# Turning gathered blocks by transposes, with the adjacency part added by VectorE and a woven VectorE order, in a two-layer graph network

## The chip, the cores and the metric

The kernel runs on one core of a Trainium2 chip. The metric is the device time of one execution in microseconds (us). Times are compared by medians of several executions; the profiles are single executions.

## What is computed

Sixteen graphs of N = 1024 nodes and 256 features pass through two layers; each layer ends in a layer norm of the sum with its input. Layer 0 is one attention head with batch norms. The change lies in layer 1, which has four heads and the 0/1 adjacency `adj`, sparse in these inputs:

```python
coefs_adj = softmax(adj)                      # the same for all heads
def head(...):                                # for each of the 4 heads
    fts = inputs @ W
    f1 = fts @ w1h + b1h
    f2 = fts @ w2h + b2h
    logits = f1[:, :, None] + f2[:, None, :]
    coefs_logits = softmax(leaky_relu(logits, 0.2) + bias_mat)   # bias_mat: -1e9 where adj is 0
    coefs = ah * coefs_logits + (1.0 - ah) * coefs_adj
    vals = coefs @ fts + bh
    return elu(vals + inputs)
out = layernorm(x + mean over heads)
```

## The kernel before, in words

Layer 0 runs first (to about 900 us of the profile), then layer 1; the constants of layer 1 (`constants1`) are made in pieces during layer 0.

Layer 1 does not multiply by the full matrices. For each graph it lists which nodes are joined to small blocks of target nodes, fetches just those rows of x, and gathers. A graph has K = 8 groups of 128 target nodes, each five blocks (NB) of QB = 25 nodes plus three shared "last" rows. For a block, `gather` (L1817, TensorE) makes `pu`: 125 rows of 256, that is 25 weighted sums for each of the four heads and 25 plain sums over the neighbours (the adjacency part). ScalarE divides each row by its sum of weights (L1883, `s`). `turn` (L1889, TensorE) then turns and mixes: for each of five blocks, `s` is the weight operand and the constant MX (125 x 100) the moving one, so that one product gives, with features down and the 25 nodes of each head across, alpha times the head's rows plus (1 - alpha) times the adjacency rows. ScalarE copies the 128 x 500 result `pt` to `sT` (`turned`, L1899). `linear` (L1912) multiplies `sT` by the heads' weights W1s; VectorE adds x as it evicts (`add`, L1920), ScalarE takes exponentials (`exps`, L1926), VectorE makes elu and the sum over heads (`sum`, L1933 to L1941), and `mean` (L1948), `squares` (L1955), `span`, `power` (POOL), `close` (L1976) and `store` are the layer norm. All matrices are float32; a float32 matrix product is two TensorE instructions, a float32 transpose one.

A unit is one group and one half: two heads in `linear`, one half of the features in `turn`. There are 16 units per graph and 256 in all. The order of instructions on every engine is written out by hand, in one loop over units (`for n in range(-EARLY, len(units) + 12)`): iteration n issues different steps of different units, for example `add` of unit n-6, `turn` and `turned` of n-3, `linear` of n-5, `gather` of n. [...]

Beside the units stands the work that prepares the next graphs ("sides"). It is put at fixed iterations relative to a graph's first unit, by the tables AT, AT0 and AT1, and comes in four parts that `stand(part, n)` issues: 0 VectorE work, 1 TensorE work and what leads to it, 2 what follows (ScalarE, DMAs), 3 the weights of gathered rows (`weigh`). The steps that matter here: `words` and `worded` (TensorE `pc`, ScalarE's copy L325, VectorE's sum L331), `pick` and `picked` (48 and 8 small products into `po`, L1520, then VectorE L1530), `turn`, `residual` and `beside` of the graph (`pz`, L1690; VectorE's copy of `fs`, L1707), `norm`, `factors`, `raised` (VectorE makes `f`, L1750; ScalarE's exponentials from it, L1756 to L1761) and `scale` (eight ScalarE instructions, L1737). Most small TensorE results of the sides share two PSUM buffers (pool `ps_s`, tag "s"); `pt` has one buffer, `pv` two, `pu` three.

The body of the loop:

```python
do(n - 9, "power")
do(n - 6, "add")
stand(0, n)
do(n - 6, "exps")
do(n - 3, "turn", "turned")
do(n - 1, "invert")
do(n - 1, "norm")
stand(2, n)
...
do(n - 5, "linear")
...
stand(3, n)
do(n - 6, "sum")
do(n - 7, "squares")
```

Of the kernel before, what the change touches and what calls it, by code (L numbers as in the profile page):

```python
# [12 lines left out]
I32 = mybir.dt.int32  # L13
# [14 lines left out]
def kernel(  # L28
# [184 lines left out]
    MX = cpool.tile([P, H, QB], F32, name="MX")  # L213
    ibits = cpool.tile([P, QB], I32, name="ibits")
# [16 lines left out]
    def constants1(wp):  # L231
# [4 lines left out]
        for oc in range(C):  # L236
# [4 lines left out]
        MY = wp.tile([P, H, QB], F32, name="MY")  # L241
        nc.vector.tensor_tensor(
            MX, ident[:, 0 : H * QB].rearrange("p (h q) -> p h q", h=H),
            al_bc.unsqueeze(2).to_broadcast([P, H, QB]), ALU.mult,
        )
        nc.vector.tensor_tensor(
            MY, ident[:, H * QB : QR].unsqueeze(1).to_broadcast([P, H, QB]),
            om_bc.unsqueeze(2).to_broadcast([P, H, QB]), ALU.mult,
        )
        nc.vector.tensor_tensor(MX, MX, MY, ALU.add)  # L250
        yield
        bits = wp.tile([P, QB], F32, name="bits")
        for i in range(QB):
# [9 lines left out]
            pick, ident[:, LO : LO + NB * QB].rearrange("p (q n) -> p n q", n=NB),  # L263
# [6 lines left out]
        rest = wp.tile([P, 3], F32, name="rest1")  # L270
        nc.vector.tensor_copy(rest[:, 0:LO], ident[:, 0:LO])
        nc.vector.tensor_copy(rest[:, LO:3], ident[:, P - 1 : P])
        last = wp.tile([P, K, 3], F32, name="last")
        nc.vector.tensor_tensor(
            last, rest.unsqueeze(1).to_broadcast([P, K, 3]),
# [35 lines left out]
        nc.sync.dma_start(W1s[0:1, 0], bias1[0:1])  # L311
# [714 lines left out]
    def dense(arm):  # L1026
# [25 lines left out]
        class Graph:  # L1052
# [157 lines left out]
            def spread(self):  # L1210
# [7 lines left out]
                ar = pk.tile([H * K, P], F32, tag="ar", name=f"ar_{self.b}", bufs=2)  # L1218
# [191 lines left out]
    with ExitStack() as l1:  # L1410
# [9 lines left out]
        class Lists:  # L1420
# [19 lines left out]
            def worded(self, hf):  # L1440
# [4 lines left out]
                words_copied(self.wd, self.pc, hf)  # L1445
                words_summed(self.wl, self.pc, hf)
# [16 lines left out]
            def placed(self):  # L1463

                b, pp = self.b, self.pp
                nc.vector.tensor_tensor(most, most, pp[:, K, :], ALU.max)
                pi = pk.tile([P, K, NQ], I32, tag="pi", name=f"pi_{b}", bufs=1)
                nc.vector.tensor_copy(pi, pp[:, 0:K, :])
                nc.vector.tensor_scalar(pi, pi, 15, None, ALU.bitwise_and)
                self.hi = pk.tile([P, K, NQ], FP16, tag="hi", name=f"hi_{b}", bufs=1)  # L1470
                nc.vector.tensor_tensor(self.hi, pp[:, 0:K, :], pi, ALU.subtract)
                nc.vector.tensor_copy(low[:, :, 0:NQ], pi)
# [15 lines left out]
            def high(self, part):  # L1488
# [3 lines left out]
                for i in range(4 * part, 4 * part + 4):  # L1492
# [3 lines left out]
                    )  # L1496

            def higher(self):
# [6 lines left out]
                )  # L1505
                nc.vector.tensor_tensor(
# [18 lines left out]
            def picked(self):  # L1525
# [7 lines left out]
                )  # L1533
                with nc.allow_low_precision(reason="one whole number and zeros"):
# [3 lines left out]
                nc.vector.tensor_scalar(  # L1538
# [630 lines left out]
```

## Time and profile before

| what | value |
|---|---|
| median of 3 executions (lowest, highest) | 2237.07 us (2195.85, 2263.55) |
| the profiled execution, and its span | 2269.36 us, 2267.5 us |
| TensorE products busy (PE) | 2058.0 us, 91% of the span |
| VectorE busy (DVE) | 1836.3 us, 81% |
| ScalarE busy (ACT) | 1453.9 us, 64% |
| GpSimd busy (POOL) | 1130.0 us, 50% |
| granted TensorE clock, mean over the span | 0.934 of full |
| `turn` L1889, products | 2560 instructions, 350.2 us, 286 ns each |
| `turned` L1899, ScalarE's copy | 256, 144.2 us, 563 ns each |
| `add` L1920, VectorE | 256, 175.1 us, 684 ns each |

A row of a group of instructions reads: line, engine, operation, out<-in with the program's names, shape, count; then busy time, the mean of one, and the idle time of the engine just before them with what released it. In a timeline a row reads: start, duration, engine, line, operation, number of instructions, and in brackets the idle time before it. A wait reads: engine, line, releaser, total time, times, longest.

### The profile page before, as it was taken

What the parts mean: (1) busy time and instruction counts of PE and PEld (TensorE: products, weight loads), DVE (VectorE), ACT (ScalarE), POOL (GpSimd) and SP (SyncE); (2) the same over time, 40 slices, a digit from 0 to 9 for tenths busy, and PEclk for the clock granted to TensorE, in tenths of its full rate; (3) what the DMA queues carried; (4) which work ended last, traced back from release to release, by engine and by line L of the source; (5) the groups of instructions that cost most, each with busy time, mean ns of one, the idle gap of its engine ahead of it and who ended that gap; (6) DMA issues with size and microseconds to landing.
All of it is one profiled execution on the core that took longest, in us unless ns stands there. A gap on an engine that the chain in (4) does not pass through costs nothing. (4 is left out here: it accounts for less than half of the span.)

```text
span 2267.5 us, 35993 instructions
## 1 busy us (share of the span) xinstructions
PE 2058.0 (91%) x12152; PEld 1594.8 (70%) x12152; DVE 1836.3 (81%) x4480; ACT 1453.9 (64%) x3192; POOL 1130.0 (50%) x1115
## 2 busy tenths in 40 slices
PE   7988799998699955999999999999999999999996
PEld 5846544444344434788888888888888888888885
DVE  3447999987599955889889889889889889889785
ACT  1236767665477733676776776776767767767674
POOL 1010266444140005666766757667667657666571
PEclk9997899998799966999999999999999999999998
DMA  7999479999997216765765756766756756756551
GB/s 237 319 180 214 108 173 219 186 161 203 177 226 186 93 59 217 194 168 182 194 170 171 197 169 173 196 165 172 203 161 164 215 155 170 208 164 169 132 143 33
DMA packets 321157, 398.42 MB, mean 176 GB/s; under 512 B 171791, under 2 KB 268099, under 8 KB 310595
## 3 DMA queue, kind: packets, MB, share of 16 engines
q1 hardware_dynamic: 268555, 250.01, 45.1%
q0 software_dynamic: 51840, 145.61, 26.4%
q8 instruction: 99, 1.62, 0.3%
q10 hardware_dynamic: 568, 0.40, 0.2%
q14 instruction: 95, 0.78, 0.1%
HBM read 326.70 MB, written 102.78 MB: 189 GB/s over the span
## 5 line engine op out<-in xcount | busy, mean ns | idle before, releaser
L1595 POOL DMA_INDIRECT xc<-xe_dram,ix x640 | 686.7, 1073 | 211.2 <-issue 182.2
L1912 PE MATMUL pv<-W1s,sT 128*128 128x256 f32 x2048 | 508.4, 393 | 0.4 <-ACT sT L1906 0.4
L887 PE MATMUL pa<-em,wh 128*128 128x512 f32 x1024 | 457.4, 605 | 10.4 <-DVE em L845 10.4
L1912 PEld LDWEIGHTS pv<-W1s,sT 128*128 128x128 f32 x2048 | 383.9, 198 | 45.1 <-ACT sT L1906 0.8
L1889 PEld LDWEIGHTS pt<-MX,s 125*128 125x128 f32 x2560 | 349.4, 203 | 29.0 <-ACT sT L1899 8.5
L887 PEld LDWEIGHTS pa<-em,wh 128*128 128x128 f32 x1024 | 195.8, 194 | 244.2 <-issue 240.1
L1889 PE MATMUL pt<-MX,s 125*128 125x100 f32 x2560 | 350.2, 286 | 4.3 <-ACT sT L1899 1.9
L1817 PE MATMUL pu<-xc,w 128*125 128x256 f32 x1280 | 346.7, 390 | 0.0
L1883 ACT ACTIVATE s<-pu,z 125x256 f32<-125x256 f32 x640 | 261.2, 474 | 79.7 <-DVE z L1875 53.3
L1926 ACT ACTIVATE m<-v,neg 128x512 f32<-128x512 f32 x256 | 183.9, 718 | 197.7 <-DVE v L1920 154.8
L97 POOL COPY mark<-em 1x1 f32<-1x1 f32 x48 | 162.4, 3384 | 224.3 <-DVE em L845 224.3
L1817 PEld LDWEIGHTS pu<-xc,w 128*125 128x125 f32 x1280 | 232.4, 192 | 34.4 <-issue 6.1
L1899 ACT COPY sT<-pt 128x500 f32<-128x500 f32 x256 | 144.2, 563 | 113.3 <-PE pt L1889 113.2
L1969 POOL TENSOR_TENSOR ors<-ors,mhalf 128x1 f32<-128x1 f32 x128 | 110.8, 866 | 196.4 <-DVE ors L1963 195.1
L839 ACT ACTIVATE e<-e,v,u 128x1024 f32<-128x1024 f32 x128 | 158.2, 1237 | 77.2 <-DVE e L833 73.0
L833 DVE SCALAR_TENSOR_TENSOR e<-e 128x1024 f32<-128x1024 f32 x128 | 155.3, 1214 | 59.2 <-ACT e L826 59.2
L826 ACT ACTIVATE e<-eb,c,s 128x1024 f32<-128x1024 f32 x128 | 157.5, 1232 | 54.8 <-DMA eb<-ec_dram 51.9
L1920 DVE TENSOR_TENSOR v<-pv,x 128x512 f32<-128x512 f32 x256 | 175.1, 684 | 16.1 <-PE pv L1912 15.9
L845 DVE TENSOR_TENSOR em<-e,mt 128x1024 f32<-128x1024 f32 x128 | 156.0, 1218 | 1.3 <-ACT e L839 1.3
L1690 PE MATMUL pz<-IW,h 128*128 128x136 f32 x512 | 89.9, 308 | 68.6 <-DVE fs L1707 38.1
L1690 PEld LDWEIGHTS pz<-IW,h 128*128 128x128 f32 x512 | 77.5, 205 | 83.5 <-issue 44.7
L853 DVE TENSOR_TENSOR sm<-sm,e 128x1024 f32<-128x1024 f32 x96 | 116.9, 1218 | 0.0
(331 smaller groups left out, 3276.1 us busy)
## 6 DMA issues: line engine op xcount, KB each, us to landing
x<-in_x_dram SPq DMA_DIRECT2D x32, 1024.0 KB
adj<-in_adj_dram POOLq DMA_DIRECT2D x64, 512.0 KB
A<-u_dram SPq DMA_DIRECT2D x128, 250.0 KB
rw<-adj SPq DMA_DIRECT2D x30, 1024.0 KB
xe_dram<-x SPq DMA_DIRECT2D x16, 1060.0 KB
h_dram<-hb SPq DMA_DIRECT2D x16, 1024.0 KB
h<-h_dram SPq DMA_DIRECT2D x16, 1024.0 KB
out_dram<-o SPq DMA_DIRECT2D x128, 128.0 KB
```

Of the source, the lines that this page charges most:

```text
L97: tc.keep_in_program_order(nc.gpsimd.tensor_copy(self.mark, data))
L826: nc.scalar.activation(e, ebs[b], AF.Identity, bias=c1[:, k, b : b + 1], scale=s1[:, k : k + 1])
L839: nc.scalar.activation(e, e, AF.Exp, bias=v2[:, k : k + 1], scale=u2[:, k : k + 1])
L887: nc.tensor.matmul(acc[b, hf, oc].rearrange("p k q -> p q k"), wh[b][:, k, oc * P : (oc + 1) * P], ems[b, k][:, hf * HALF : (hf + 1) * HAL ...
L1595: nc.gpsimd.indirect_dma_start(out=self.xc[:, i, :], out_offset=None, in_=xe_dram[g.b % 2], in_offset=bass.IndirectOffsetOnAxis(ap=g.l.ix[ ...
L1690: nc.tensor.matmul(pz[:, oc, :], self.h[:, oc, k * P : (k + 1) * P], IW[:, oc, :], start=True, stop=True,)
L1817: nc.tensor.matmul(pu[0:QR, 0:F], c.w[:, k].rearrange("p h q -> p (h q)"), c.xc[:, k, 0:F], start=(i == 0), stop=(i == len(OF[q]) - 1),)
L1883: nc.scalar.mul(f.s[0:QR, i], f.pu[i][0:QR, 0:F], f.z[0:QR, i : i + 1])
L1889: nc.tensor.matmul(self.pt[:, :, :, i], self.first.s[0:QR, i, self.hp * P : (self.hp + 1) * P], MX[0:QR], start=True, stop=True,)
L1912: nc.tensor.matmul(self.pv[:, hh, :], self.first.sT[:, fc, self.hp * HP + hh, :], W1s[:, fc, self.hp * HP + hh, :], start=(fc == 0), stop= ...
L1920: nc.vector.tensor_tensor(self.v2, self.pv, self.g.x[:, self.it].unsqueeze(1).to_broadcast([P, HP, F]), ALU.add)
L1926: nc.scalar.activation(self.m, self.v2, AF.Exp, bias=neg1, scale=1.0)
```

## The change

**Turn.** Four of the five blocks are no longer multiplied by MX. They are transposed on TensorE (against the identity), into a `pt` whose rows are four heads and the adjacency part, 25 nodes by four blocks. ScalarE copies the adjacency part to `sM` (128 x 100), and `turned` is now a VectorE addition of `sM` to the four heads as they leave PSUM (128 x 400). The fifth block still uses MX, once for both halves of the features, on every second unit (`turn_fifth`, into a `ps_s` buffer `pf`; copied by ScalarE in `turned_fifth`).

**Mixing weights.** (1 - alpha) goes into W1s and the bias, alpha / (1 - alpha) into the divisors of the four blocks (`part`, one small ScalarE instruction per unit) and into MX. `spread` uses a permutation matrix `by_block` in place of the identity. These constants are made in `constants1`.

**Moved to ScalarE.** `mean`, `means` and the scaling of the last rows in `gathered`.

**Order.** Many VectorE steps yield between their instructions, and `woven` issues the threads `weigh`, side part 0 and `sum` in turn, one instruction of each. In the loop `invert`, `turn` and `turned` come straight after `add`; `linear` and `turn_fifth` come before the woven part. In `weigh` the product comes ahead of the bit mask. For graph 1 the side step `turn` has its own times. Side steps that free PSUM come first in part 0.

The diff, cut to its core:

```diff
@@ -238,16 +240,40 @@
...
-        MY = wp.tile([P, H, QB], F32, name="MY")
+        om = wp.tile([P, 2, H], F32, name="om")
+        nc.vector.tensor_scalar(om[:, 0], om_bc, 0.0, FAINT, ALU.is_equal, ALU.mult)
+        nc.vector.tensor_tensor(om[:, 0], om[:, 0], om_bc, ALU.add)
+        nc.vector.reciprocal(om[:, 1], om[:, 0])
+        nc.vector.tensor_tensor(om[:, 1], om[:, 1], al_bc, ALU.mult)
         nc.vector.tensor_tensor(
             MX, ident[:, 0 : H * QB].rearrange("p (h q) -> p h q", h=H),
-            al_bc.unsqueeze(2).to_broadcast([P, H, QB]), ALU.mult,
+            om[:, 1].unsqueeze(2).to_broadcast([P, H, QB]), ALU.mult,
         )
         nc.vector.tensor_tensor(
-            MY, ident[:, H * QB : QR].unsqueeze(1).to_broadcast([P, H, QB]),
-            om_bc.unsqueeze(2).to_broadcast([P, H, QB]), ALU.mult,
+            MX, MX, ident[:, H * QB : QR].unsqueeze(1).to_broadcast([P, H, QB]), ALU.add,
         )
-        nc.vector.tensor_tensor(MX, MX, MY, ALU.add)
...
+        nc.vector.tensor_reduce(most_of[:, 0:1], apart.rearrange("p h q -> p (h q)"), AX.X, ALU.add)
+        nc.vector.tensor_reduce(most_of[:, 1:2], ident[:, H * QB : P], AX.X, ALU.add)
+        nc.vector.tensor_tensor(part, most_of[:, 0:1], most_of[:, 1:2], ALU.add)
...
@@ -308,7 +331,13 @@
...
         for fc in range(C):
             nc.vector.tensor_tensor(W1s[:, fc], W1s[:, fc], wl, ALU.subtract)
-        nc.sync.dma_start(W1s[0:1, 0], bias1[0:1])
+            nc.vector.tensor_tensor(
+                W1s[:, fc], W1s[:, fc], om[:, 0].unsqueeze(2).to_broadcast([P, H, F]), ALU.mult
+            )
+        nc.vector.tensor_tensor(
+            wl[0:1], bias1[0:1], om[0:1, 0].unsqueeze(2).to_broadcast([1, H, F]), ALU.mult
+        )
+        nc.sync.dma_start(W1s[0:1, 0], wl[0:1])
...
@@ -1443,6 +1472,7 @@
...
+                yield
                 words_summed(self.wl, self.pc, hf)
 
             def used(self):
@@ -1531,13 +1566,15 @@
...
+                nc.vector.tensor_scalar(
+                    V[:, NB:8].rearrange("p g a -> p (g a)"), po[:, 320:344], in8[:, 0:1], None, ALU.mult
+                )
+                yield
                 with nc.allow_low_precision(reason="one whole number and zeros"):
                     nc.vector.tensor_reduce(
                         V[:, 0:NB], t.rearrange("p g q a -> p g a q"), AX.X, ALU.add
                     )
-                nc.vector.tensor_scalar(
-                    V[:, NB:8].rearrange("p g a -> p (g a)"), po[:, 320:344], in8[:, 0:1], None, ALU.mult
-                )
+                yield
                 self.E = pk.tile([P, 8, 8, 16], FP16, tag="E", name=f"E_{b}", bufs=1)
                 nc.vector.tensor_tensor(
@@ -1606,15 +1643,9 @@
...
                 wi = flat.bitcast(I32)[:, a : a + (n - 1) * step + 1 : step]
-                mi = pk.tile([P, n, QB], I32, tag="mi" + self.big, name=f"mi_{self.nm}", bufs=2)
-                nc.vector.tensor_tensor(
-                    mi, wi.unsqueeze(2).to_broadcast([P, n, QB]),
-                    ibits.unsqueeze(1).to_broadcast([P, n, QB]), ALU.bitwise_and,
-                )
                 w = self.w = pk.tile(
                     [P, n, H + 1, QB], F32, tag="w" + self.big, name=f"w_{self.nm}", bufs=4 if n == NB else 2
                 )
-                nc.scalar.copy(w[:, :, H, :], mi)
                 A = g.A[self.u]
                 if self.u == K:
                     nc.vector.memset(w[:, :, 0:H, QB - 1 : QB], 0.0)
@@ -1627,10 +1658,19 @@
...
+                yield
+                mi = pk.tile([P, n, QB], I32, tag="mi" + self.big, name=f"mi_{self.nm}", bufs=2)
+                nc.vector.tensor_tensor(
+                    mi, wi.unsqueeze(2).to_broadcast([P, n, QB]),
+                    ibits.unsqueeze(1).to_broadcast([P, n, QB]), ALU.bitwise_and,
+                )
+                nc.scalar.copy(w[:, :, H, :], mi)
+                yield
                 nc.vector.tensor_tensor(
                     w[:, :, 0:H, :], w[:, :, 0:H, :],
                     xc[:, :, F1 + H : WB].unsqueeze(3).to_broadcast([P, n, H, QB]), ALU.max,
                 )
+                yield
                 nc.vector.tensor_tensor(
                     w[:, :, 0:H, :], w[:, :, 0:H, :], mi.unsqueeze(2).to_broadcast([P, n, H, QB]), ALU.mult
...
@@ -1708,7 +1748,7 @@
...
             def means(self, hf):
                 mn = self.mv[:, 0, hf * KH : (hf + 1) * KH]
-                nc.vector.tensor_scalar(mn, mn, -1.0 / F, None, ALU.mult)
+                nc.scalar.mul(mn, mn, -1.0 / F)
...
@@ -1743,10 +1783,13 @@
+                yield
                 nc.vector.tensor_tensor(self.f, self.f, self.fs[:, :, 1], ALU.add)
+                yield
                 nc.vector.tensor_tensor(
                     self.f, self.f, self.rs[:, 1].unsqueeze(2).to_broadcast([P, K, 2 * H]), ALU.mult
                 )
+                yield
                 nc.vector.tensor_tensor(
@@ -1792,18 +1835,16 @@
...
             def spread(self):
                 self.pb = ps_s.tile([K * H, 2, P], F32, tag="s", name=f"pA_{self.b}")
-                nc.tensor.transpose(self.pb[:, 0], self.e.rearrange("p k h -> p (k h)"), ident)
-                nc.tensor.transpose(self.pb[:, 1], self.e2.rearrange("p h k -> p (h k)"), ident)
+                for i, e in enumerate(
+                    (self.e.rearrange("p k h -> p (k h)"), self.e2.rearrange("p h k -> p (h k)"))
+                ):
+                    nc.tensor.matmul(self.pb[:, i], e, by_block, start=True, stop=True)
 
             def spreaded(self):
                 n = NB * QB
                 self.ar = pk.tile([K * H, P], F32, tag="ar", name=f"ar_{self.b}", bufs=2)
-                nc.scalar.copy(
-                    self.ar[:, 0:n].rearrange("p (n q) -> p q n", n=NB),
-                    self.pb[:, 0, LO : LO + n].rearrange("p (q n) -> p q n", n=NB),
-                )
-                nc.scalar.copy(self.ar[:, n : n + LO], self.pb[:, 1, 0:LO])
-                nc.scalar.copy(self.ar[:, n + LO : P], self.pb[:, 1, P - 1 : P])
+                nc.scalar.copy(self.ar[:, 0:n], self.pb[:, 0, 0:n])
+                nc.scalar.copy(self.ar[:, n:P], self.pb[:, 1, n:P])
...
@@ -1827,7 +1868,7 @@
...
-                nc.vector.tensor_scalar(self.s[0:QR], self.pu[0:QR, 0:F], z[0:QR], None, ALU.mult)
+                nc.scalar.mul(self.s[0:QR], self.pu[0:QR, 0:F], z[0:QR])
 
...
@@ -1879,28 +1921,48 @@
...
+                lo, hi = (0, 3) if self.hp == 0 else (3, 4)
+                nc.scalar.mul(f.z[0:QR, lo:hi], f.z[0:QR, lo:hi], part[0:QR])
                 for i in self.blocks():
                     nc.scalar.mul(f.s[0:QR, i], f.pu[i][0:QR, 0:F], f.z[0:QR, i : i + 1])
 
             def turn(self):
 
-                self.pt = ps_t.tile([P, H, QB, NB], F32, tag="t", name=f"pt_{self.nm}")
-                for i in range(NB):
+                f = self.first
+                self.pt = ps_t.tile([P, H + 1, QB, NB - 1], F32, tag="t", name=f"pt_{self.nm}")
+                for i in range(NB - 1):
                     nc.tensor.matmul(
-                        self.pt[:, :, :, i],
-                        self.first.s[0:QR, i, self.hp * P : (self.hp + 1) * P],
-                        MX[0:QR], start=True, stop=True,
-                    )
+                        self.pt[:, :, :, i], f.s[0:QR, i, self.hp * P : (self.hp + 1) * P],
+                        ident[0:QR, 0:QR].rearrange("p (h q) -> p h q", h=H + 1),
+                        start=True, stop=True, is_transpose=True,
+                    )
+                if self.hp == 0:
+                    f.sT = pk.tile([P, C, H, SW], F32, tag="sT", name=f"sT_{self.nm}", bufs=2)
+                self.sM = pk.tile([P, (NB - 1) * QB], F32, tag="sM", name=f"sM_{self.nm}", bufs=2)
+                nc.scalar.copy(self.sM, self.pt[:, H].rearrange("p q n -> p (q n)"))
...
             def turned(self):
-                f, u = self.first, self.it
-                if self.hp == 0:
-                    f.sT = pk.tile([P, C, H, P], F32, tag="sT", name=f"sT_{self.nm}", bufs=2)
-                nc.scalar.copy(
-                    f.sT[:, self.hp, :, LO : LO + NB * QB],
-                    self.pt.rearrange("p h q n -> p h (q n)"),
-                )
+                rows = self.first.sT[:, self.hp, :, LO:SW].rearrange("p h (e j) -> p h e j", e=2)
+                nc.vector.tensor_tensor(
+                    rows[:, :, :, 0 : 2 * QB],
+                    self.pt[:, 0:H].rearrange("p h q n -> p h (q n)").rearrange("p h (e j) -> p h e j", e=2),
+                    self.sM.rearrange("p (e j) -> p e j", e=2).unsqueeze(1).to_broadcast([P, H, 2, 2 * QB]),
+                    ALU.add,
+                )
+
+            def turn_fifth(self):
                 if self.hp == 1:
+                    self.pf = ps_s.tile([P, C, H, QB], F32, tag="s", name=f"pf_{self.nm}")
+                    for fc in range(C):
+                        nc.tensor.matmul(
+                            self.pf[:, fc], self.first.s[0:QR, NB - 1, fc * P : (fc + 1) * P],
+                            MX[0:QR], start=True, stop=True,
+                        )
+
+            def turned_fifth(self):
+                if self.hp == 1:
+                    f, u, m = self.first, self.it, LO + 2 * QB
+                    nc.scalar.copy(f.sT[:, :, :, m : m + QB], self.pf)
                     sl = self.g.sl[:, :, :, 3 * u : 3 * u + 3]
                     nc.scalar.copy(f.sT[:, :, :, 0:LO], sl[:, :, :, 0:LO])
                     nc.scalar.copy(f.sT[:, :, :, P - 1 : P], sl[:, :, :, LO:3])
@@ -1933,10 +1995,13 @@
...
                 nc.vector.scalar_tensor_tensor(v, self.m, 1.0, v, ALU.min, ALU.max)
+                yield
                 nc.vector.tensor_tensor(v, g.acc, v, ALU.add)
+                yield
                 o = self.o = pk.tile([P, F], F32, tag="o", name=f"o_{nm}", bufs=4)
 
                 nc.vector.scalar_tensor_tensor(o, g.x[:, it, 0:F], float(H), v[:, 0], ALU.mult, ALU.add)
+                yield
                 self.mv = pk.tile([P, 2], F32, tag="omv", name=f"omv_{nm}", bufs=5)
                 nc.vector.tensor_tensor_reduce(
...
@@ -1945,9 +2010,7 @@
...
             def mean(self):
                 if self.hp == 1:
-                    nc.vector.tensor_scalar(
-                        self.mv[:, 0:1], self.mv[:, 0:1], -1.0 / F, None, ALU.mult
-                    )
+                    nc.scalar.mul(self.mv[:, 0:1], self.mv[:, 0:1], -1.0 / F)
...
@@ -2010,6 +2073,7 @@
...
         }
+        AT1['turn'] = (-18, -18, -17, -15, -15, -14, -14, -13)
 
...
@@ -2025,7 +2089,7 @@
...
                 first[n] += [each(f, *args)]
-                early[n + 1] += [each(then, *args)]
+                freed[n + 1] += [each(then, *args)]
 
...
@@ -2089,35 +2153,52 @@
...
+        def in_turn(steps):
+            for step in steps:
+                parts = step()
+                if parts is not None:
+                    yield from parts
+                yield
+
+        def woven(*threads):
+            threads = [in_turn(steps) for steps in threads]
+            while threads:
+                threads = [t for t in threads if next(t, t) is not t]
...
         with tc.manual_schedule():
 
             for n in range(-EARLY, len(units) + 12):
                 do(n - 9, "power")
                 do(n - 6, "add")
-                stand(0, n)
+                do(n - 1, "invert")
+                do(n - 3, "turn", "turned")
                 do(n - 6, "exps")
-                do(n - 3, "turn", "turned")
-                do(n - 1, "invert")
                 do(n - 1, "norm")
+                do(n - 5, "linear")
+                do(n - 3, "turn_fifth")
+                woven(
+                    *of(3, n), *of(0, n),
+                    [units[n - 6].sum] if 0 <= n - 6 < len(units) else [],
+                )
+                do(n - 3, "turned_fifth")
                 stand(2, n)
                 do(n - 10, "close")
                 do(n - 11, "store")
-                do(n - 5, "linear")
                 if 0 <= n < len(units):
                     units[n].gather(0)
                 stand(1, n)
                 if 0 <= n < len(units):
                     units[n].gather(1)
-                do(n - 7, "mean")
                 do(n - 8, "span")
-                stand(3, n)
-                do(n - 6, "sum")
-                do(n - 7, "squares")
+                do(n - 7, "mean", "squares")
...
```

## Prediction

> **What bounds the kernel now.** The profiled execution took 2269.4 us around a span of 2267.5; the median of the runs shown is 2237.07. I make every sum against the span and carry the difference over to the median. First I read the window table for the middle of layer 1 (1000 to 2100 us) and, for transposes, for 100 to 180 us of layer 0.
>
> ```profile
> core 0: us, PE busy (x) PEld busy (x) DVE busy (x) ACT busy (x) POOL busy (x), PEclk, DMA share, GB/s
> 1000.00:2100.00 1100.00, 1052.04 (x7013) 928.52 (x7013) 967.07 (x2696) 788.82 (x2098) 730.18 (x770) 0.96 0.64 178
> 100.00:180.00 80.00, 72.84 (x420) 45.37 (x419) 42.36 (x200) 31.18 (x57) 10.42 (x17) 0.98 1.20 184
> ```
>
> TensorE is busy 96% of layer 1, VectorE 88%, ScalarE 72%. A graph is 16 units; L1920 runs once a unit, 204 times in the window, so a unit takes 5.39 us and a graph 86.3. Of a graph's 86.3 VectorE works 75.9. What it waits for:
>
> ```profile
> DVE wl L331 <- ACT wd L325: 56.5, 13, 4.4
> DVE ptt L1530 <- PE po L1520: 33.6, 12, 3.4
> DVE v L1920 <- PE pv L1912: 6.8, 12, 1.3
> DVE v L1935 <- ACT m L1926: 5.0, 13, 0.4
> ```
>
> (Line, releaser, total us, times, longest.) With 3.7 us at L1684 and small ones it waits 107.7 us, 8.4 per graph, nearly all at two places that come once a graph: the copy of `pc` and the product `po`. The timelines show what stands in front. VectorE, then TensorE, around the second:
>
> ```profile
> 1501.10 0.68 DVE L1920 TENSOR_TENSOR v<-pv,x 128x512 f32<-128x512 f32 x1
> 1505.12 0.49 DVE L1530 TENSOR_TENSOR ptt<-po,in 128x320 f32<-128x320 f32 x1 [3.34 <-PE po L1520]
> ```
>
> ```profile
> 1500.13 4.96 PE L1520 MATMUL po<-hA,B 128*128 128x64 f16 x48
> 1504.91 1.20 PE L1817 MATMUL pu<-xc,w 128*125 128x256 f32 x2
> 1505.90 2.28 PE L1889 MATMUL pt<-MX,s 125*128 125x100 f32 x10
> ```
>
> So the kernel is bound by TensorE with VectorE about ten per cent behind; a change that shortens TensorE is soon stopped by VectorE, and by what VectorE waits for.
>
> [...] VectorE stood 3.34 us at L1530 while L1875, L1963 and L1935, next in its order, ran only after it. [...]
>
> **The change, part by part.**
>
> *Turn on TensorE, removed.* L1889's ten instructions a unit take 1.09 us at full clock (1208.13 to the start of what follows at 1209.22). Four transposes with their weight loads take 0.43 in layer 0:
>
> ```profile
> 100.43 0.60 PE L453 MATMUL px<-ident,x 128*128 128x128 f32 x4
> 100.86 1.96 PE L474 MATMUL pw<-WX,xT 128*128 128x266 f32 x8
> ```
>
> The new turn has four, plus the fifth block by MX every second unit (four instructions, 0.43, so 0.22 a unit). Saved 1.09 - 0.65 = 0.44 a unit, 7 us a graph. The transposes write every fourth float where layer 0 writes adjacent ones; L1889 already writes every fifth[...], so I take 0.43, with 0.87 (its own rate for four blocks) as the upper end.
>
> *Add on VectorE.* One 128x400 addition a unit (`turned`). No row has this size. L1530 takes 0.491 us at 320, L1920 0.684 at 512: 0.57 between them. [...] Behind an independent instruction the next starts some 0.07 sooner than the end (L1933 at 1500.49, 0.68 long, L1920 at 1501.10), so 0.5 a unit: +7.9 a graph.
>
> *Moved to ScalarE.* L1948 (8 x 132 ns), L1711 (2 x 164) and L1830 (484) a graph, less the same overlap: -1.0 on VectorE.
>
> *Woven order.* A successor that reads its predecessor's output starts 0.72 us after it (L1935 at 1507.90, L1936 at 1508.62), an independent one 0.61: 0.11 to 0.12 per pair. Counting pairs in the trace's instruction list gives 683 in the window, 54 a graph; the new instruction order leaves about 15. -39 x 0.12 = -4.6.
>
> VectorE without waits: 86.3 - 8.4 = 77.9, then +7.9 - 1.0 - 4.6 = 80.2 a graph. TensorE: it waited some 4 us (27.2 and 17.7 us in the window at L1690) and is at 86.3 - 7 = 79.3. ScalarE: 61 - 16 x 0.56 (L1899) + some 0.75 a unit for the copy `sM`, the factor `part`, half the fifth's copy and the means: about 64, no bound. Constants: some 30 small VectorE instructions in layer 0, where VectorE works 53%; nothing, and under 10 us once if the cover fails.
>
> *The new wait.* `turned` on VectorE waits for ScalarE's `sM`, which waits for TensorE's transposes; it stands ahead of the whole woven part (weigh, side work, sum), so every later VectorE instruction is queued behind it. In a common iteration TensorE and ScalarE are ready. Twice a graph they are not.
>
> (a) After `pick`. `pf` needs a PSUM buffer that VectorE frees about 3.1 us into the iteration (the copy of `fs`, in program order). Then TensorE runs 0.43 (`pf`), 0.87 (gather), 4.8 (`po`), 0.43 to 0.99 (gather; after `po` the clock halves: the turn at 1505.90 took 2.08, not 1.09), 0.44 to 0.88 (transposes), and ScalarE 0.3: ready at 10.3 to 11.3. VectorE comes there at about 6.2. Wait 4.1 to 5.1, say 5 with semaphores, where L1530 waited 2.6 on average.
>
> (b) After `norm`. ScalarE's part, before:
>
> ```profile
> 1517.62 0.25 ACT L1756 ACTIVATE x<-f 128x32 f32<-128x32 f32 x1
> ...
> 1518.29 4.04 ACT L1737 ACTIVATE x<-x,rs 128x256 f32<-128x256 f32 x8
> 1522.23 0.58 ACT L1976 ACTIVATE o<-o,ors 128x256 f32<-128x256 f32 x1
> 1522.72 0.28 ACT L325 CAST wd<-pc 128x160 int32<-128x160 f32 x1
> ```
>
> From the first `raised` to the end of L1976's slot 5.1 us, and `sM` 0.3 behind it: 5.4 after `f` is ready. The weave makes `f` the last VectorE instruction of its iteration; from there VectorE has only L1963 0.13, L1920 0.68, L1875 0.23 before `turned`. Wait 4.4 to 4.8 [...]. That replaces the wait at L331, 4.4, which comes too late to wait then.
>
> Sum: 80.2 + 5 + 4.8 + 0.3 for small ones (0.4 to 3 possible) = 90.3 a graph against 86.3. Fourteen graphs of this kind: +56. The last but one took 69.6 with VectorE at 57.3: +7.9 - 0.6 - 2.5 and wait (b) come to about 72, +2; the last (TensorE 52.4 of 59.4 us) gains 2 to 3. Together +56: 2323 on the span, 2293 on the median.
>
> **Rivals.** *R1, faster: the weave hides the waits.* If TensorE and ScalarE run far enough ahead, VectorE works 80.2 a graph: -6.1 x 14 = -85, about 2150. For it: TensorE's new slack of 7 us. Against: both waits start from VectorE's own results (`fs`, `f`), so running ahead does not help. It decides once both waits together are below 6.1 us a graph; for over 2% faster (3.2 a graph) below 2.9.
> *R2, half hidden:* `fs` is free earlier, or `f` comes before the end of the weave, and the two waits sum to 6 to 8: 86 to 88 a graph, about 2250.
> *R3, the change does not do what it says:* strided transposes run at L1889's rate. TensorE is back at 86, the `po` chain longer by 0.44: about +0.65 a graph over the likeliest, 2302; up to 2340 if TensorE's losses and VectorE's waits add.
> *R4, more waits:* `turned` also waits where ScalarE has a block of four squares or an exponential ahead of `sM`; +2 to 3 a graph, about 2330.
>
> **How the numbers follow.** Likeliest 0.58, its own range 2265 to 2335 (waits (a) and (b) 8.3 to 12 us). R1 0.12, R2 0.14, R3 0.06, R4 0.10. This measurement tells about 2% from no change: 2192 to 2282. Faster: R1's 0.12. Within: R2's 0.13, 0.08 of the likeliest, 0.02 of R3 and R4: 0.23. Slower: 0.65. The range 2235 to 2345 leaves out R1 and the top of R4, under 0.2.
>
> **What would show it.** Right: `turned` about 0.57 us; four transposes about 0.43; TensorE's busy share in layer 1 down to about 85%; the wait list headed by `turned` for `sM` with some 10 us a graph, longest near 5, and L331 and L1530 nearly gone from it; a graph of 90. Wrong: `turned` waits under 6 us a graph (R1, R2), or transposes at 0.87 (R3), or waits spread over many iterations (R4). The sum would also fall if far fewer than 39 dependent pairs go, or if the half-clock stretches after `po` become longer.

## The result, and the profile after

The changed kernel takes 2384.97 us (median of 4), the kernel before 2219.52 in the same comparison: ratio 1.0835, 95% interval 1.0796 to 1.0874. The forecast was 2293, about 1.025, in a range up to 2345. The direction was right, the size a third of what came. Some executions of one kernel are some per cent longer than the others, at a lower granted clock (before, beside one experiment: 2263.39 us at 0.942, 2207.81 at 0.953); the ratios, here and below, leave those out, and the medians do not, so that a ratio need not be the quotient of two medians.

Layer 1 holds nearly all of it. From the first addition of graph 0 to that of graph 15 pass 1438.9 us (873.4 to 2312.3), before 1279.1 (914.5 to 2193.6): +159.8. A graph takes 97.3 us where it took 86.3, forecast 90.3. (The profiled execution of before, 2269.36 us, entered layer 1 some 41 us later than that of after, so the two spans differ by less than the medians.)

The parts first. L1946 is the addition in `turned`, L1942 the copy `sM`, L1917 `invert`. From the page's groups, then the window table and the waits (VectorE's, then TensorE's) of 1000 to 2200 us, in which L1982, the addition of x, runs 197 times:

```profile
L1946 DVE TENSOR_TENSOR sT<-pt,sM 128x400 f32<-128x400 f32 x256 | 145.3, 567 | 149.1 <-ACT sM L1942 148.0
```

```profile
1000.00:2200.00 1200.00, 975.90 (x6016) 806.09 (x6015) 982.06 (x2677) 811.50 (x2433) 690.86 (x741) 0.94 0.56 159
```

```profile
DVE sT L1946 <- ACT sM L1942: 121.9, 115, 4.6
DVE z L1917 <- PE pu L1858: 78.4, 49, 4.1
DVE wl L360 <- ACT wd L354: 6.8, 13, 0.5
```

```profile
PE pf L1957 <- DVE ix L1596: 61.2, 12, 5.1
PE pz L1730 <- ACT sT L1965: 30.1, 13, 2.4
PE pf L1957 <- DVE fs L1747: 27.2, 25, 1.7
PE ptl L1876 <- DVE fs L1747: 19.2, 12, 1.6
PE pp L1484 <- DVE act L364: 18.2, 13, 1.4
```

Per graph (x 16/197) VectorE is busy 79.8 us and TensorE 79.3. Both are as forecast (80.2 and 79.3). But a graph takes 97.3: each engine stands idle 18 us, VectorE for TensorE and ScalarE, TensorE mostly for VectorE; none of the waits listed is for a DMA. Before, TensorE was busy 96% of layer 1; now neither engine is over 82%. So no engine's work sets the period, but the waits of the engines for each other.

Where in the graph? The next table is worked out from the traces: start of one addition of x to the next, for each of the 16 iterations of the loop, mean of graphs 2 to 12. "Waits" are VectorE's gaps over 0.09 us. The last column is an experiment told below.

| iteration | before | after | waits in after | units ahead, no pf |
|---|---|---|---|---|
| 0, 1, 2 | 4.87, 4.69, 5.45 | 5.62, 4.77, 5.53 | 0.5 | 5.80, 4.80, 5.48 |
| 3 (after `pick`) | 9.07 | 10.64 | 4.8 | 7.48 |
| 4, 5 | 3.87, 4.04 | 3.91, 3.97 | 0.1 | 3.91, 3.98 |
| 6 (after `norm`) | 9.40 | 9.88 | 4.6 | 9.88 |
| 7, 8, 9 | 3.75, 4.39, 4.34 | 6.18, 5.43, 5.42 | 1.8, 0.8, 1.2 | 4.27, 4.82, 5.46 |
| 10, 11, 12 | 4.39, 5.31, 5.01 | 4.59, 6.37, 5.12 | 0, 1.2, 0 | 4.58, 5.74, 5.12 |
| 13 | 9.18 | 10.10 | 1.7 | 8.25 |
| 14, 15 | 3.92, 4.63 | 4.53, 5.26 | 0.1, 0.6 | 4.40, 4.72 |
| sum | 86.3 | 97.3 | 17.5 | 88.7 |

The two waits that were forecast are there with their sizes (4.8 and 4.6 us; 5 and 4.8 forecast). Most of the first falls at `invert`, which waits for a gather behind `po`:

```profile
1351.12 0.17 DVE L1917 RECIPROCAL z<-pu 125x1 f32<-125x1 f32 x1 [3.81 <-PE pu L1858]
1351.83 0.57 DVE L1946 TENSOR_TENSOR sT<-pt,sM 128x400 f32<-128x400 f32 x1 [0.54 <-ACT sM L1942]
```

Beside them stand 8.1 us of waits in other iterations, 4.7 at `turned` and 2.5 at `invert`, where the forecast had 0.3. Iterations 6 and 7 show how one wait makes the next. VectorE, then TensorE:

```profile
1370.10 0.58 DVE L1946 TENSOR_TENSOR sT<-pt,sM 128x400 f32<-128x400 f32 x1 [4.63 <-ACT sM L1942]
1370.59 0.67 DVE L1657 TENSOR_TENSOR w<-A,xc 128x500 f32<-128x500 f32 x1
1371.18 0.22 DVE L1596 TENSOR_TENSOR ix<-pl,spare 128x64 uint32<-128x64 f32 x1
...
1376.23 0.17 DVE L1917 RECIPROCAL z<-pu 125x1 f32<-125x1 f32 x1 [0.88 <-PE pu L1858]
1376.93 0.57 DVE L1946 TENSOR_TENSOR sT<-pt,sM 128x400 f32<-128x400 f32 x1 [0.54 <-ACT sM L1942]
```

```profile
1364.56 1.90 PE L1974 MATMUL pv<-W1s,sT 128*128 128x256 f32 x8
1371.54 1.15 PE L1957 MATMUL pf<-MX,s 125*128 125x100 f32 x4 [5.08 <-DVE ix L1596]
1372.48 1.96 PE L1858 MATMUL pu<-xc,w 128*125 128x256 f32 x4
```

VectorE waits 4.63 us for `sM` behind ScalarE's scale block. L1596, which frees a side buffer, stands behind that wait. TensorE needs the buffer for `pf`, waits 5.08 us, and starts again at half speed: 0.94 us to the next start where the same four products take 0.42 without a wait. The window table has the granted clock (after the five busy times) at 0.50 there:

```profile
1371.50:1374.40 2.90, 2.86 (x9) 2.05 (x10) 2.90 (x7) 2.37 (x8) 2.45 (x2) 0.50 0.95 220
```

So the gather behind it is late, and VectorE waits again. It is what the prediction read at L1530, where VectorE stood 3.34 us and what was next in its order ran only after it, taken one step further: what stands behind a waiting instruction is also what frees buffers (here L1596 starts 1.08 us after L1946, which waited 4.63).

### The profile page after: what moved, and what is told of

It is laid out like the page before. It is cut to its first block, busy times and chain, and to the rows that moved or that the text cites. A ratio compares the mean times of both kernels' runs of the same rounds, so it can differ in the third digit from the quotient of the medians.

```text
span 2384.4 us, 34612 instructions
## 1 busy us (share of the span) xinstructions
PE 1985.5 (83%) x11160; PEld 1464.1 (61%) x11160; DVE 1898.2 (80%) x4579; ACT 1522.3 (64%) x3736; POOL 1118.5 (47%) x1115
## 4 chain that ended last, share of the span: by engine, by line
PE 44%; DVE 27%; ACT 11%; issue 9%; DMA 5%; POOL 3%; DVEq 0%; SPq 0%; ACTq 0%; POOLq 0%
PE pa L916 19%; PE pu L1858 5%; PE po L1555 3%; PE pw L503 3%; DVE w L1657 3%; ACT x L1777 2%; DVE acc L1995 2%; POOL xc L1632 2%; PE pt L1934 2%; DVE v L1982 2%; DVE sT L1946 2%; DVE v L1997 2%; ACT m L1988 2%; DVE w L1669 2%; ACT s L1927 1%
## 5 line engine op out<-in xcount | busy, mean ns | idle before, releaser
L1632 POOL DMA_INDIRECT xc<-xe_dram,ix x640 | 712.4, 1113 | 218.1 <-issue 186.4
L916 PE MATMUL pa<-em,wh 128*128 128x512 f32 x1024 | 448.7, 597 | 10.5 <-DVE em L874 10.5
L1858 PE MATMUL pu<-xc,w 128*125 128x256 f32 x1280 | 370.1, 411 | 0.0
L1946 DVE TENSOR_TENSOR sT<-pt,sM 128x400 f32<-128x400 f32 x256 | 145.3, 567 | 149.1 <-ACT sM L1942 148.0
L2032 POOL TENSOR_TENSOR ors<-ors,mhalf 128x1 f32<-128x1 f32 x128 | 75.1, 587 | 380.3 <-DVE ors L2026 377.8
L1942 ACT COPY sM<-pt 128x100 f32<-128x100 f32 x256 | 60.0, 235 | 277.5 <-PE pt L1934 277.4
L868 ACT ACTIVATE e<-e,v,u 128x1024 f32<-128x1024 f32 x128 | 158.2, 1237 | 89.5 <-DVE e L862 85.2
L1730 PE MATMUL pz<-IW,h 128*128 128x136 f32 x512 | 95.8, 316 | 111.2 <-ACT sT L1965 32.3
L1982 DVE TENSOR_TENSOR v<-pv,x 128x512 f32<-128x512 f32 x256 | 174.4, 681 | 0.0
L1934 PE MATMUL pt<-ident,s 125*128 125x125 f32 x1024 | 167.0, 287 | 6.9 <-ACT s L1927 3.2
L1957 PE MATMUL pf<-MX,s 125*128 125x100 f32 x512 | 84.4, 291 | 96.0 <-DVE ix L1596 66.2
L1934 PEld LDWEIGHTS pt<-ident,s 125*128 125x128 f32 x1024 | 136.0, 150 | 46.1 <-DVE sT L1946 12.6
L1730 PEld LDWEIGHTS pz<-IW,h 128*128 128x128 f32 x512 | 78.3, 208 | 133.4 <-issue 38.8
## 6 DMA issues: line engine op xcount, KB each, us to landing
adj<-in_adj_dram POOLq DMA_DIRECT2D x64, 512.0 KB, 12.5
```

The costliest lines, as they stand in the source:

```text
L868: nc.scalar.activation(e, e, AF.Exp, bias=v2[:, k : k + 1], scale=u2[:, k : k + 1])
L916: nc.tensor.matmul(acc[b, hf, oc].rearrange("p k q -> p q k"), wh[b][:, k, oc * P : (oc + 1) * P], ems[b, k][:, hf * HALF : (hf + 1) * HAL ...
L1632: nc.gpsimd.indirect_dma_start(out=self.xc[:, i, :], out_offset=None, in_=xe_dram[g.b % 2], in_offset=bass.IndirectOffsetOnAxis(ap=g.l.ix[ ...
L1730: nc.tensor.matmul(pz[:, oc, :], self.h[:, oc, k * P : (k + 1) * P], IW[:, oc, :], start=True, stop=True,)
L1858: nc.tensor.matmul(pu[0:QR, 0:F], c.w[:, k].rearrange("p h q -> p (h q)"), c.xc[:, k, 0:F], start=(i == 0), stop=(i == len(OF[q]) - 1),)
L1934: nc.tensor.matmul(self.pt[:, :, :, i], f.s[0:QR, i, self.hp * P : (self.hp + 1) * P], ident[0:QR, 0:QR].rearrange("p (h q) -> p h q", h=H ...
```

## Experiments

Ratios are to the kernel before, timed on the same chip beside each experiment. It took 2211 to 2269 us there, so ratios, and not times, are to be compared from one experiment to another; the changed kernel was not timed again beside them. "A graph" is the period in the one execution profiled; 86.3 before, 97.3 after.

**Which part costs.** Order alone: all edits but the turn, its constants, spread and `pf`.

> The new order, the yields and the steps moved to ScalarE, but the turn of before: five products with MX, ScalarE's 128x500 copy, no addition on VectorE, no pf, the old mixing weights and spread. Theory A (the cost is that VectorE stands in line at the turned addition for ScalarE and TensorE, and that TensorE stands in line at pf): no addition to wait at and no pf, so TensorE bounds again and a graph takes about 86 us as before; 2190 to 2240 us, same. Theory B (the cost is the addition's work on VectorE): also about the same as before. Theory C (the woven order itself costs, whatever the turn): slower than before by most of the 165 us, 2330 or more.

2299.86 us, ratio 1.0387 (1.0345 to 1.043), a graph 92.1: between what theories A and B and what theory C expected. The new order costs by itself, about half of the whole. VectorE's work fell as forecast (busy 72.4 us a graph; 77.9 - 1.0 - 4.6 was 72.3), but it waits for exponentials and gathers:

```profile
DVE acc L1947 <- ACT m L1940: 93.2, 76, 5.1
DVE v L1949 <- ACT m L1940: 71.2, 74, 2.6
DVE z L1889 <- PE pu L1831: 44.5, 23, 2.8
```

Turn alone: the turn with its constants in the old loop.

```diff
-                do(n - 3, "turn", "turned")
+                do(n - 3, "turn", "turned", "turn_fifth", "turned_fifth")
```

> The new turn (transposes, addition on VectorE, fifth block, mixing weights, spread) in the old order, without yields; the fifth block's product and copy straight after the turn. Theory A: the addition stands behind the side work, whose two waits (po, pc) come first as before and cover it, but every unit still adds 0.5 us to VectorE: 85.8 of work with the dependent pairs plus 8 to 11 of waits, 94 to 97 us a graph, 2330 to 2375 us. Theory B: 7.9 us a graph, about 94, 2335 us. Theory C: no slower than before, about 2220 us.

2522.29 us, 1.1392 (1.1346 to 1.1438), a graph 105.8: worse than any theory had it, and worse than the whole change. The old order puts `pf` where VectorE has just begun the side work that frees its buffer; TensorE stands there 160 us of 1100, in three stalls a graph of 3.8 to 6.0 us. After each of the nine such stalls between 1000 and 1330 us it has half the clock (0.50) for 5.3 to 5.6 us (the mean granted clock of layer 1 is 0.86; TensorE is busy 85 us a graph where it is busy 79 in the changed kernel):

```profile
PE pf L1943 <- DVE fs L1736: 104.2, 21, 6.0
PE pf L1943 <- DVE wl L360: 55.9, 10, 5.6
```

The same, but `pf` comes last in the iteration and takes turns with `pt` in one buffer (two edits at once):

> The turn alone in the old order, but the fifth block's product comes last in the iteration and takes turns with pt in pt's buffer. In the turn alone TensorE stood 160 us in a window of 1100 at pf, waiting for VectorE to free a side buffer. If pf's place is what made it 105.8 us a graph: 91 to 96 us, 2300 to 2380 us. If the addition on VectorE and its wait for sM do it: over 100 us, 2440 us or more.

2535.12 us, 1.1113 (1.0956 to 1.127), a graph 102.2. The waits at `pf` go, others come (TensorE's turn waits 96 us for ScalarE's copy of `pf`). So the place that `pf` had is a part, not the whole, of what the turn costs in the old order; in its new place and buffer it still holds TensorE up. The parts don't add: +5.8 for the order, +19.5 for the turn, +11 for both.

**Work or waits.** Changed kernel, ScalarE copies the heads' part and VectorE adds nothing (the adjacency part of four blocks is left out):

> The changed kernel, but ScalarE copies the four heads' part of pt straight to sT and VectorE adds nothing: the adjacency part of four of five blocks is left out. Order, transposes and pf stay. Theory A: the addition's work (7.9 us a graph) and all of its waits (9 us) go, the waits of invert for pu stay in part; 97.3 falls to 81 to 85 us a graph, 2150 to 2210 us. Theory B: only the work goes, 97.3 to 89.4 us, about 2270 us. Theory C: under 3 per cent gained, 2320 us or more.

2337.24 us, 1.0577 (1.053 to 1.0623), a graph 93.9. That is theory C. Of 7.9 us of work taken off VectorE only 3.4 came back; the rest turned into other waits (at L1917 for the gather, at the sum for exponentials). ScalarE's copy takes 0.49 us where that of `sM` took 0.24, which may be a part of it. The result speaks against the work as the bound, and against the addition as the only place to wait.

**The order's own cost.** Order alone, exponentials ahead of the turn's copy:

```diff
-                do(n - 3, "turn", "turned")
                 do(n - 6, "exps")
+                do(n - 3, "turn", "turned")
```

> The order alone again (old turn, no addition on VectorE), but ScalarE's exponentials are issued ahead of its copy of the turned blocks, as in the kernel before. In the order alone VectorE waited 164 us in a window of 1100 for the exponentials, which stood behind that copy and so behind TensorE. Theory D (the new order ties VectorE's sum to TensorE through ScalarE's queue): these waits shrink, a graph falls from 92.1 to 84 to 87 us, 2180 to 2230 us. Theory E (TensorE and VectorE wait for each other through the side work's two PSUM buffers, whatever ScalarE does): another wait takes their place, 90 to 92 us a graph, 2265 to 2300 us.

2285.4 us, 1.0095 (1.0065 to 1.0126), a graph 89.1: from 1.0387. By the ratios the exponentials' place in ScalarE's queue is most of what the order cost, by the periods half (this profile is of an execution of 2302.77 us, and a burst of TensorE in it is 1.0 us a graph longer than elsewhere, as told at the end). Then also TensorE's units (second gather, next turn) ahead of the side products:

```diff
-                do(n - 3, "turn", "turned")
+                do(n - 3, "turned")
...
-                stand(1, n)
                 if 0 <= n < len(units):
                     units[n].gather(1)
+                do(n - 2, "turn")
+                stand(1, n)
```

> The new order with the old turn and the exponentials first (89.1 us a graph), and the units' gather and turn ahead of the side products. VectorE waited 8 us a graph at invert for a gather that stood behind a side product. If that is what the order still cost: 83 to 86.5 us a graph, 0.97 to 1.0 of before. If not: 88 us or more, over 1.005.

A graph 85.2, in the shortest of four executions (2193.53 us); the median is 2231.56 us against 2227.2, without an interval, so the time is not told from before. With both queues mended the order costs nothing that shows.

**The changed kernel's small waits.** First `pf` moved to the buffer of `pt` (`ps_t`, tag "t"):

> The changed kernel, but the fifth block's product pf takes turns with pt in pt's one PSUM buffer, so that it no longer waits for, or holds up, the two buffers of the side work. Theory A with pf as the cause of the small waits: TensorE's 5 us stall at pf ahead of ix goes, and with it the waits of invert and turned in the next iterations; 3 to 5 us a graph less, 2315 to 2345 us. Theory A without it (pf then waits for the addition itself, which is as late): under 1.5 us a graph, 2365 to 2390 us. Theory B: no change.

2370.24 us, 1.0708 (1.0679 to 1.0737), a graph 95.6: a little, in iterations 3 and 7 (1.4 us each, of which iteration 11 gives 1.0 back); `pf` now waits for the addition itself (102.9 us of 1100). Then `pf` left out, ScalarE copying old values:

> The changed kernel without the fifth block's product (left out; ScalarE copies old values in its place, so the copy's time stays). If pf is what ties TensorE to VectorE (7 us a graph of waits at it): 97.3 to 91 to 94 us a graph, 1.04 to 1.06 of before, with the 5 us stall of TensorE gone. If the next side product then waits for the same buffer: 95 to 97 us, 1.07 to 1.083.

2389.3 us, 1.0636 (1.0516 to 1.0757), a graph 94.3. The stall of iteration 6 did not go: the next side product now waits for the same buffer (L1841 for L1596, 50.3 us in 12 times). Yet iteration 7 falls from 6.18 to 4.27 us: in the loop this product stands behind the first part of the gather, and `pf` stood ahead of it. Then the units ahead, as in the diff above:

> The changed kernel with TensorE's order changed alone: the second part of the gather and the next turn come ahead of the side products (po among them), so that what invert and turned wait for is not behind po. Theory A: the 4.7 us after po fall to about 1.5 (VectorE then waits for po itself), and the waits of 1 us at invert in other iterations go; 97.3 to 90 to 93 us, 1.03 to 1.055 of before. Theory E: the side products come later, so the buffers do, and TensorE waits more; 95 to 98 us, 1.07 to 1.09.

2373.27 us, 1.0521 (1.0396 to 1.0645), a graph 95.0; iterations 7 and 13 lose 1.0 and 1.9, `pf` now stalls TensorE at three places. Both:

> The changed kernel with the units' gather and turn ahead of the side products, and pf in turns with pt in pt's buffer. If the two causes are separate, 97.3 - 2.4 - 1.7 = 93 us a graph, 1.03 to 1.05 of before; if they are one tie seen twice, 95 to 97 us, 1.05 to 1.08.

2332.03 us, 1.0417 (1.0329 to 1.0504), a graph 92.1. That is what two separate causes were expected to give (93), and a little more. TensorE still waits at `pf`, now for the addition:

```profile
PE pf L1957 <- DVE sT L1946: 115.6, 72, 3.9
```

And the units ahead with `pf` left out:

> The changed kernel with the units ahead and without the fifth block's product (left out; old values are copied in its place). If separate: 97.3 - 2.4 - 3.0 = 92 us a graph, 1.02 to 1.045 of before; what is left over 80 is then the wait behind scale (4.6), po, and ScalarE's blocks. If one tie: 94 to 96 us, 1.05 to 1.07.

2266.33 us, 1.0235 (1.0155 to 1.0316), a graph 88.7: 8.6 less than the change, more than the two alone (2.4 and 3.0). The likely reading is that they hide each other: with one in place TensorE is held up at the other. This kernel also does less: eight `pf` of 0.42 us are 3.4 us of TensorE's work a graph, as much as the whole difference from the run before (92.1 to 88.7), so how much of that is the tie and how much the work is not shown. What VectorE still waits for:

```profile
DVE sT L1946 <- ACT sM L1944: 102.0, 62, 4.6
DVE wl L360 <- ACT wd L354: 6.9, 11, 0.7
DVE w_l L1652 <- DMA A_l<-v_dram: 1.6, 3, 0.8
```

More than half of that is iteration 6, the wait behind scale, untouched at 9.88 us. The gathers are gone from the list.

**Remedies that failed.** The addition behind the woven part:

> The changed kernel with three moves: the addition goes behind the woven part, so that VectorE has some 4 us of other work before it; the exponentials go ahead of the copy sM; the gather's second part goes ahead of the side products (po among them). Theory A (in-order waits at turned and invert are the cost): the 9.9 us a graph at turned and the 6.4 at invert fall to 2 to 5 together, 97.3 to 84 to 88 us, 2200 to 2255 us. Theory E: TensorE's next turn then waits for the late addition and the rest of the ring stays, 93 to 97 us, 2325 to 2385 us.

2460.93 us against 2262.08, without an interval; a graph 99.0. TensorE's next turn waits for the late addition and what stands around it, 130 us of 1100. Scale in two iterations:

```diff
-'norm': -11, 'scale': (-11, -11), 'table': -9
+'norm': -11, 'scale': (-11, -10), 'table': -9
```

> The changed kernel with ScalarE's eight scale instructions (4.0 us) in two iterations of four, for graphs 2 to 15. Theory A: the 4.6 us wait at turned behind them falls to about 2.6, the iteration after it gains 0 to 1.5; 1 to 2.5 us a graph less, 2350 to 2370 us. If that iteration is as long for another reason: under 0.5 us a graph, 2378 to 2390 us.

2487.83 us, 1.0982 (1.0858 to 1.1105), a graph 103.4. Iteration 6 becomes 1.8 us shorter and iteration 7 1.2 longer, as forecast. Iterations 10 and 11 grow by 6.8 us together, about as much as a slow burst of TensorE in iteration 10, shown at the end. A third side buffer, taken from `pv`:

> The changed kernel with a third PSUM buffer for the side work and pf, taken from pv, which then has one. Theory E (TensorE and VectorE, each with 80 us of work a graph, wait for each other in turn because TensorE's side products and pf wait for buffers that VectorE frees late): TensorE's 18 us of waits a graph fall to under 10 and the period from 97.3 to 91 to 94 us; 1.04 to 1.06 of the time before. Theory A (VectorE waits behind po, scale and ScalarE's blocks, buffers or not): 96 to 98 us, 1.075 to 1.09 of before.

2526.07 us, 1.1244 (1.1133 to 1.1356), a graph 104.0. TensorE's waits did not go, they moved to the linear product, which now waits for the addition before it:

```profile
PE pv L1974 <- DVE v L1982: 134.7, 53, 4.3
PE pv L1974 <- DVE z L1917: 46.5, 32, 2.2
```

So the run does not test the side buffers; it shows what a tie of TensorE to a late VectorE instruction is worth. All three together:

> Three together: units ahead of side products, a third side buffer (pv has one), and scale in two iterations. If the waits add up as both theories have it, 97.3 less 6 for the units, 3 for the buffer and 1.5 for scale: 86 to 89 us a graph, 0.99 to 1.03 of before. If they hide one another: 91 us or more, over 1.045.

2399.25 us, 1.0635 (1.0511 to 1.0758), a graph 96.2. The gains do not add, but the reason is not shown: the buffer taken from `pv`, which cost 6.7 us a graph alone, is one of the three, and TensorE waits for it here too (106.1 us of 1100 at `pv` for the addition of x).

**The moves alone.** Kernel before with `mean`, `means` and the last rows' scaling on ScalarE and the freeing steps first:

> The kernel before with mean, means and the scaling of the last rows on ScalarE and the side steps that free PSUM first; no new turn, no weave, the old loop. TensorE bounds and waited 3.5 us a graph at pz, half of it for the scaling of the last rows on VectorE. If the moves cost: over 1.02 of before. If they are free or help TensorE: 84 to 86.5 us a graph, 0.975 to 1.005 of before.

2194.93 us, 0.989 (0.9805 to 0.9974), a graph 84.9. The one version that comes out faster than both kernels, by a per cent, with an interval that ends just short of 1. Its window table has TensorE busy 97% of the time, so there is little more to be had while TensorE's work stays as it is:

```profile
1000.00:2100.00 1100.00, 1071.45 (x7085) 944.75 (x7083) 962.67 (x2569) 811.99 (x2275) 743.61 (x782) 0.96 0.66 179
```

## Why the prediction was wrong

- *TensorE saves 0.44 us a unit:* right. Four transposes take 0.43 (1364.13 to 1364.56), so writing every fourth float took no longer than layer 0's adjacent ones did (0.43, 100.43 to 100.86), and TensorE's busy time per graph came out at the forecast.
- *The addition, 0.57 us:* right, 567 ns, as read between L1530's 0.491 us at 320 and L1920's 0.684 at 512. *Dependent pairs, the moves, VectorE's sum:* right to half a microsecond.
- *Waits (a) and (b):* right in place and size. Of (a), 3.9 us fell at `invert`, ahead of `turned` in VectorE's order, which the text did not see; the sum is the same. That the waits of `turned` came to the 10 us a graph that were to show it right is luck: some 5.3 of them are (a) and (b), and small waits make up the rest. The step "L1946 replaces the wait at L331" held.
- *"In a common iteration TensorE and ScalarE are ready. Twice a graph they are not", and so "0.3 for small ones":* wrong. It measured 8.1 us a graph. I added the two great waits to VectorE's work and took TensorE as ready everywhere else. It was not: `pf` and the side products take buffers that VectorE frees in its woven part, behind `invert` and `turned`, so TensorE is tied to VectorE's place in the iteration, and the side products stand ahead of the gather and the turn that VectorE needs next. Shown by the run with the units ahead and `pf` moved, which keeps all the work: 5.2 of the 11 us go, and the waits outside iterations 3 and 6 fall from 8.1 to 4.7 (12.5 less 3.2 and 4.6). With `pf` left out 8.6 go, and these waits fall to 3.1 (9.4 less 1.7 and 4.6), but part of that may be the 3.4 us of work left out. Against the forecast the graph is 7.0 us too long: +7.8 for this term, -0.8 for the others together. Fourteen graphs make 98 of the 109 us by which the change was missed (165 less 56); the first graph, which took 102.2, makes 5 more.
- *The rivals:* R4 had the mechanism (more waits of `turned`) at 2 to 3 us, a third of its size, and only by ScalarE's blocks; iteration 9 may be one of these (1.2 us, the same with `pf` alone moved or left out).
- *The order as a gain of 4.6 us:* the work fell by that, but the order alone is slower. ScalarE's exponentials behind the turn's copy, and TensorE's units behind the side products, cost more than it gave. The prediction priced the weave by VectorE's queue and did not ask the same of the other two.

Open: what makes the turn dearer in the old order than both together is shown only in part (`pf`'s place, 3.6 of 19.5 us a graph, and the lower granted clock, 0.86 for 0.96), and of the runs with the new order or the new turn that kept scale where it is none shortened iteration 6 by more than 0.4 us (9.50 to 9.99 us there, 9.88 in the changed kernel).

## What to carry over

When a change leaves two engines with nearly equal work, the period can lie well above the larger sum (here 97 us for 80 and 79): write out, for one iteration of each kind, what each engine's next instruction waits for, and follow the buffers as well as the data, since a buffer freed late in one engine's order was here a wait early in another's. A new small product in a shared pool of two buffers is such a tie, and the stall can cost far more than the product (5.1 us for one of 0.42). Put what another engine waits for ahead of what nobody waits for, on every queue, before weighing cycles.

## What was not expected of the hardware

After each of the twelve stalls of 5.1 us at `pf` between 1000 and 2200 us of the changed kernel TensorE ran at half the clock (0.50) for 4.1 to 5.9 us (added up from the granted clock in slices of 0.25 us), so such a stall cost more than its length (four products in 0.94 us instead of 0.42 after the one at 1371.54). After two shorter stalls at `pf`, of 1.1 and 1.7 us, the clock stood at 1.00 for the 2.8 us that followed; elsewhere it was at 0.51 from 1396.1 to 1399.1 us, soon after a stall of only 2.3 (L1730 at 1395.15), so the length of one stall does not settle it. The mean granted clock in layer 1 fell from 0.96 to 0.94, and to 0.86 in the turn alone, where the stalls at `pf` come three times a graph.

A burst of 32 small products (`pc`, L347) takes 0.78 us from its first start to its last in before, in after (two of the 32 bursts in each 0.85 and 0.87) and in most runs. With scale in two iterations its second burst in a graph stretched to as much as 9.4 us, with gaps between products that wait for nothing the profile shows:

```profile
1436.46 0.70 PE L347 MATMUL pc<-add,rw 128*128 128x6 bf16 x11
1438.45 0.20 PE L347 MATMUL pc<-add,rw 128*128 128x6 bf16 x2 [1.28 <-issue]
1439.20 0.29 PE L347 MATMUL pc<-add,rw 128*128 128x6 bf16 x6 [0.55 <-issue]
```

In the order with the exponentials first it took up to 2.6 us, on the same chip, on which two other kernels timed with it had 0.78; on another chip it took 5.3 us once without `pf`, and 4.1 once with all three edits. Its cause stays open; it is why the total of the run with scale in two iterations says little about scale.
